# A graph network on one core: where an attention stage keeps its target rows and its masks, and how its head loads

## The chip, the cores and the metric

The program runs on one core of a Trainium2 chip, as one launch. Its time is the device time of that launch in microseconds, and three timed runs stand for it. The engines that matter are TensorE (PE, with its weight loads PEld), VectorE (DVE), ScalarE (ACT), GpSimd (POOL) and SyncE (SP). Each works through its own instructions in order; they meet in semaphores. Here POOL does nothing but issue row gathers by index, and SP and ACT also issue the other transfers. [...]

## What is computed

Two graph layers over 12,500 nodes of 128 features and 400,000 edges sorted by target. The first is a relational convolution of two sub-layers with ten relations, the second an attention layer with four heads of 32 features:

```python
h = jnp.maximum(_layernorm(x, axis=-1), 0.0)
x = x + _L0_gnn_ref(h, node_vec, edge_weight, edge_attr_42, ...)   # two relational sub-layers
h = jnp.maximum(_layernorm(x, axis=-1), 0.0)
x = x + _L1_gnn_ref(h, edge_index, W_l, W_r, att, bias)

def _L1_gnn_ref(x, edge_index, W_l, W_r, att, bias):
    xl, xr = (x @ W_l).reshape(n, H, C), (x @ W_r).reshape(n, H, C)
    xj, xi = xl[src], xr[dst]
    score = jnp.einsum('ehc,hc->eh', leaky_relu(xi + xj, 0.2), att)
    ex = jnp.exp(score - segment_max(score, dst)[dst])
    alpha = ex / (segment_sum(ex, dst)[dst] + 1e-16)
    out = segment_sum(alpha[..., None] * xj, dst)
    return out.reshape(n, H * C) + bias
```

All of it is in float32.

## The kernel before

The edges are cut into G = 125 groups of 3200: 128 partitions with J = 25 consecutive edges each. As the targets are sorted, a group touches at most 128 neighbouring nodes, and a half row (13 or 12 edges, `HALVES`) at most two of them. A check in the head confirms this, and a flag chooses between `sorted_edges` (which runs here) and a general path. The stages follow one another:

- **Head** (`first_table`, lines 327 to 449): 98 tiles of 128 nodes. Each is normalised, turned, and multiplied by the ten relation weights in three matmul groups; DVE copies the first and third part out of PSUM, ACT the second, and ACT's queue stores 640 KB per tile to the table `t1_d`. The rows of x come as 26 loads `xq` of four tiles (line 349), each into a tile of its own, and all are issued on SP's queue at the start, with the whole target list `dst_i` after the fourth (354) and the whole source list `src_i` after the seventh (356). Per four tiles, SP also stores `xb` (x plus a bias, two buffers, 445 and 446) and `hT`. From tile LEAD = 12 on, one step of `analysis` (185 to 325) goes into each tile; it reads `dst_i`.
- **Relational sub-layers** (`layer1`, `layer2`): per group, 25 gathers on POOL and sums on DVE and ACT.
- **Attention** (lines 871 to 1096): a loop of turns t = 0 to G, in an order that is written out by hand (`manual_schedule`). A turn works on three groups: it loads for group t, scores group a = t-1, and sums group q = t-3.

In an attention turn the order of issue is: 25 gathers `xs` (479) of group t, into one of five buffers; on SP `load(t)`: a cell of the target list (473), from it the row number, then the 128 target rows `xr` (906), the rows `db` (908), the penalties `pen` (910), and `x2` (1051). Then the first two `first_xr` copies `z` on ACT (931). `score(0)` on DVE: a predicated copy (937) that puts a partition's second target row over the first where the mask `mk` says so, the sum with the gathered rows (939), leaky relu times attention (941), and the reduction to scores (943). `flow` on DVE and PE carries maxima across partitions (967 to 982). `score(1)`; `end` finishes group q-1 and SP stores it (1020 to 1027). `add_up` takes maxima off the scores (988 to 994), exponentiates on ACT (998), and then for each of five slices of five edges: the product `xw` on DVE (1002), a small copy of the weights on ACT (1005), the one-hot `s` on DVE (1007), five matmuls into `po` (1011). `score(2)`, `score(3)`; `maxima` (949 to 960). Then `prepare(t)`: DVE compares `db` into `st` (916) and makes the masks `mk` (919), ACT copies `pk` (922), PE makes the target rows `xn` from `xr` and `st` (925). Last `take`: ACT copies the finished sums out of `po` (1036).

The places matter. `xn` is one PSUM bank, written by PE and read by both ACT (931) and DVE (937). `z` has two buffers in PSUM. One further bank, `bank`, holds the index row `iotap` that the one-hots compare with, and the two `exps` that ACT writes and DVE (1002) and ACT (1005) read. `mk` lies in SBUF. `xw` and `s` have four buffers each (pool "go", line 878), with five tiles of each per turn.

Of the kernel before, what the change touches and what calls it, by code (L numbers as in the profile page):

```python
# [18 lines left out]
P = 128  # L19
J = 25  # L20
# [6 lines left out]
def kernel(  # L27
# [299 lines left out]
    def first_table():  # L327

        Q = 4
        LEAD = 12  # L330
# [5 lines left out]
        with tc.tile_pool(name="vw", bufs=1) as wp, tc.tile_pool(name="vx", bufs=1) as xp, \  # L336
# [5 lines left out]
            b2b = bcast_row(wp, b2, "b2b")  # L342
            dst_i = ap.tile([P, G, J], I32, name="dst_i")
            xs = []
            for q, ts in enumerate(quads):
                n = len(ts)
                r = starts[ts[0]]
                xq = xp.tile([P, Q, D], F32, name=f"xq{q}")
                nc.sync.dma_start(xq[:, :n, :], x[r:r + n * P, :].rearrange("(k p) d -> p k d", p=P))
# [57 lines left out]
            for i in range(3):  # L407
                norm(i)
            for i in range(2):
                turn(i)  # L410
                relu(i)
            look = analysis(ap, pp, dst_i)
            for i, (q, k) in enumerate(tiles):
                hT = hTs[q][:, k, :]
                ts = tp.tile([P, R * D], F32, name="ts")

                def part(c):
                    n = min(512, R * D - c)
                    ps = psum.tile([P, 512], F32, name="ps")
                    nc.tensor.matmul(ps[:, :n], hT, wall[:, c:c + n], start=True, stop=True)  # L420
# [5 lines left out]
                nc.vector.tensor_copy(*one)  # L426
                nc.scalar.copy(*more[0])
                relu(i + 2)
                scales()
                norm(i + 3)  # L430
                for m in more[1:]:
                    nc.vector.tensor_copy(*m)
                n = len(quads[q])
                stats(q + 2, k)
                if k == n - 1:
                    for kk in range(n, Q):
                        stats(q + 2, kk)
                if i >= LEAD:
                    next(look, None)
                r = starts[quads[q][k]]  # L440
                nc.scalar.dma_start(tv[r:r + P, :], ts)
                if k == n - 1:
                    r = starts[quads[q][0]]
                    xb = xp.tile([P, Q, D], F32, name=f"xb{q % 2}")
                    nc.vector.tensor_add(xb[:, :n, :], xs[q][:, :n, :], b2b[:, None, :].to_broadcast([P, n, D]))
                    nc.sync.dma_start(xb_d[r:r + n * P, :].rearrange("(k p) d -> p k d", p=P), xb[:, :n, :])
                    nc.sync.dma_start(hT_d[:, r:r + n * P], hTs.pop(q)[:, :n, :].rearrange("d k p -> d (k p)"))
            for _ in look:
                pass


    def sorted_edges():
# [4 lines left out]
        with tc.tile_pool(name="sd", bufs=1, space=DRAM) as sd, tc.tile_pool(name="sk", bufs=1) as sk:  # L457
# [403 lines left out]
            with tc.tile_pool(name="gk", bufs=1) as kp, tc.tile_pool(name="gx", bufs=5) as xp, \  # L861
                    tc.tile_pool(name="gw", bufs=2) as wp, tc.tile_pool(name="gs", bufs=3) as sp, \
                    tc.tile_pool(name="go", bufs=4) as op, \
# [7 lines left out]
                exps = [bank[:, k * P:k * P + H * J].rearrange("p (h j) -> p h j", h=H) for k in (1, 2)]  # L871
                nc.vector.tensor_copy(iotap, iota)
# [20 lines left out]
                def flat(t):  # L893
                    return t.rearrange("p h j -> p (h j)")
# [18 lines left out]
                def prepare(g, xr, db):  # L913
# [3 lines left out]
                    mk = wp.tile([P, J], F32, name="mk")  # L917
# [8 lines left out]
                    return xn, mk.bitcast(I32), flat(pk)  # L926
# [69 lines left out]
                def sums(g, xs, sc, po, before):  # L996
# [3 lines left out]
                    for j0 in range(0, J, JW):  # L1000
                        xw = op.tile([P, JW, H, AW], F32, name="xw")
# [4 lines left out]
                        s = op.tile([P, JW, P], F32, name="s")  # L1006
                        nc.vector.tensor_tensor(s, iotap[:, None, :].to_broadcast([P, JW, P]),  # L1007
                                                dst_b[:, g, j0:j0 + JW, None].to_broadcast([P, JW, P]),
                                                op=OP.is_equal)
# [32 lines left out]
                with tc.manual_schedule():  # L1042
                    for t in range(G + 1):
# [33 lines left out]
                        score(1)  # L1077
                        if q >= 1:
                            end(q - 1)
# [7 lines left out]
                        if t < G:  # L1087
                            xn[t] = prepare(t, xr.pop(t), dbs.pop(t))
# [440 lines left out]
```

## Time and profile before

| | us |
|---|---|
| median of three runs | 14032.24 (14024.25 to 14067.41) |
| the profiled execution, its own time | 14041.59 |
| its span, first to last instruction | 14039.8 |
| head, 0 to about 283 | 283 |
| first sub-layer, 283 to 4893 | 4610 |
| second sub-layer, 4893 to 9340 | 4447 |
| attention, 9340 to 14040 | 4700 |
| one attention turn (from one first predicated copy at 11622.84 to the next at 11659.18) | 36.34 |

In a row of the timeline stand the start in us from the beginning of the span, the duration, the engine, the line, the operation with what it writes and reads, how many are merged, and in brackets the idle time before it with what ended it. "issue" and "remote" there mean that the profile doesn't show what ended the wait. A wait's row gives the engine and line that waited, what for, the total in us, how often, and the longest. Rows of a stretch give the busy time of each engine in it. The ends of matmuls are modelled.

### The profile page before, as it was taken

The page shows a single profiled execution, that of the slowest core. Times are in us where ns is not written, and L with a number is a line of the kernel's source. Part 1 is how long each engine was busy: PE and PEld are TensorE (multiplying, and loading weights), DVE is VectorE, ACT ScalarE, POOL GpSimd, SP SyncE. Part 2 cuts the span into 40 slices and gives each one's busy share as a digit, 9 for nine tenths or more (in the row PEclk, how much of TensorE's full clock was granted, in tenths as well). Part 3 has the DMA queues.
Part 4 walks back from the last instruction along what each step waited for, and adds up shares of the span by engine and source line. Part 5 has one row for each costly group of instructions (what it writes and reads, how often), then busy time and mean ns, then how long its engine had stood idle before and what let it go on. Part 6 is the DMA issues. An engine that isn't in the chain of part 4 may idle for free.

```text
span 14039.8 us, 68433 instructions
## 1 busy us (share of the span) xinstructions
PE 3446.7 (25%) x12832; PEld 2310.3 (16%) x12832; DVE 9212.9 (66%) x12638; ACT 2298.5 (16%) x6975; POOL 9120.0 (65%) x9384
## 2 busy tenths in 40 slices
PE   6122222222222211111111111112333333333333
PEld 3011111111111100000000000002222222222223
DVE  7566666666666565555555565656777777777777
ACT  2233223333232200000000000001111111111111
POOL 1666666666666577777777666655666666666664
PEclk8555555555555555555555555555666666666666
DMA  8222222222222211111111111111222222222221
GB/s 274 76 82 85 84 81 86 83 83 86 85 81 86 70 56 54 54 54 54 54 54 54 53 55 54 55 49 50 56 56 57 56 56 57 56 52 56 57 56 40
DMA packets 595938, 964.56 MB, mean 69 GB/s; under 512 B 190432, under 2 KB 397866, under 8 KB 595498
## 3 DMA queue, kind: packets, MB, share of 16 engines
q0 software_dynamic: 300000, 621.40, 16.5%
q1 hardware_dynamic: 280090, 273.82, 6.2%
q10 hardware_dynamic: 15408, 64.89, 1.2%
q14 instruction: 336, 2.75, 0.1%
q8 instruction: 104, 1.70, 0.0%
HBM read 758.60 MB, written 200.85 MB: 68 GB/s over the span
## 4 chain that ended last, share of the span: by engine, by line
issue 28%; DVE 27%; POOL 19%; another core or an unknown queue 12%; PE 6%; ACT 5%; DMA 2%; SPq 0%; DVEq 0%; ACTq 0%; POOLq 0%
POOL xs L496 14%; POOL xs L479 5%; ACT y L528 3%; DVE z L939 2%; DVE lr L941 2%; DVE y L516 2%; PE po L1011 2%; DVE xw L1002 2%; DVE sc L943 2%; DVE r L534 2%; DVE z L937 2%; DVE s L1007 1%; DVE r L519 1%; DMA xs<-xl_d,src_i 1%
## 5 line engine op out<-in xcount | busy, mean ns | idle before, releaser
L496 POOL DMA_INDIRECT xs<-t_d,idx x6250 | 6146.7, 983 | 2821.1 <-issue 1867.4
L479 POOL DMA_INDIRECT xs<-xl_d,src_i x3125 | 2971.4, 951 | 1690.9 <-issue 913.0
L519 DVE TENSOR_REDUCE r<-y 128x256 f32<-128x3072 f32 (+1 forms) x375 | 2102.9, 5608 | 30.5 <-DVE y L516 0.5
L516 DVE TENSOR_TENSOR y<-xs,wk 128x3072 f32<-128x3072 f32 (+1 forms) x375 | 1324.4, 3532 | 368.5 <-DMA xs<-t_d,idx 237.0
L1011 PE MATMUL po<-xw,s 128*128 128x132 f32 x6250 | 1101.5, 346 | 1323.5 <-issue 1030.4
L1011 PEld LDWEIGHTS po<-xw,s 128*128 128x128 f32 x6250 | 1019.5, 252 | 1385.8 <-issue 1054.3
L553 PE MATMUL ps<-r,s 128*128 128x128 f32 x1000 | 305.6, 461 | 3528.0 <-issue 1905.8
L714 PE MATMUL pt<-wall,hT 128*128 128x512 f32 x750 | 640.9, 991 | 1391.0 <-remote 865.0
L807 DVE TENSOR_TENSOR x<-sm,ac 128x128 f32<-128x128 f32 x125 | 36.4, 291 | 1420.0 <-DMA xl_d<-ts 1030.5
L528 ACT ACTIVATE y<-xs,wk 128x128 f32<-128x128 f32 x3000 | 933.6, 488 | 148.4 <-issue 92.2
L937 DVE COPY_PREDICATED z<-mk,xn 128x896 f32<-128x896 int32 x500 | 491.1, 982 | 561.5 <-ACT z L931 284.2
L553 PEld LDWEIGHTS ps<-r,s 128*128 128x128 f32 x1000 | 231.9, 322 | 3654.9 <-issue 1974.7
L1002 DVE TENSOR_TENSOR xw<-xs,bank 128x640 f32<-128x640 f32 x625 | 508.9, 814 | 304.4 <-remote 164.0
L1007 DVE TENSOR_TENSOR s<-bank,dst_b 128x640 f32<-128x640 f32 x625 | 515.4, 825 | 170.0 <-issue 89.9
L931 ACT COPY z<-xn 128x896 f32<-128x896 f32 x500 | 395.0, 812 | 909.7 <-DVE lr L941 689.8
L939 DVE TENSOR_TENSOR z<-xs,z 128x896 f32<-128x896 f32 x500 | 497.8, 996 | 39.3 <-DMA xs<-xl_d,src_i 22.4
L941 DVE SCALAR_TENSOR_TENSOR lr<-z,att 128x896 f32<-128x896 f32 x500 | 495.2, 990 | 17.1
L943 DVE TENSOR_REDUCE sc<-lr 128x28 f32<-128x896 f32 x500 | 493.9, 988 | 17.1
L553 PE MATMUL ps<-s,r 128*128 128x128 f32 x1000 | 305.5, 461 | 806.6 <-issue 433.3
L718 DVE TENSOR_TENSOR ts<-pt,xb 128x128 f32<-128x128 f32 x125 | 35.5, 284 | 697.6 <-ACT tr L650 649.5
L714 PEld LDWEIGHTS pt<-wall,hT 128*128 128x128 f32 x750 | 209.8, 320 | 1701.9 <-remote 942.9
L534 DVE TENSOR_REDUCE r<-y 128x256 f32<-128x3072 f32 x125 | 411.9, 3295 | 0.0
(211 smaller groups left out, 5834.7 us busy)
## 6 DMA issues: line engine op xcount, KB each, us to landing
xs<-t_d,idx POOLq DMA_INDIRECT x6250
t_d<-ts SPq DMA_DIRECT2D x125, 640.0 KB
m<-in_edge_attr_dram SPq DMA_DIRECT2D x125, 525.0 KB
t_d<-ts ACTq DMA_DIRECT2D x98, 640.0 KB
xs<-xl_d,src_i POOLq DMA_INDIRECT x3125
db<-drow_d SPq DMA_DIRECT2D x125, 128.0 KB
xl_d<-ts SPq DMA_DIRECT2D x125, 66.0 KB
at<-hT_d SPq DMA_DIRECT2D x125, 64.0 KB
```

What stands on the lines that cost most here:

```text
L479: nc.gpsimd.indirect_dma_start(out=xs[:, j, :], out_offset=None, in_=table, in_offset=bass.IndirectOffsetOnAxis(ap=ids[:, j:j + 1], axis=0))
L496: nc.gpsimd.indirect_dma_start(out=x[:, j, :], out_offset=None, in_=table, in_offset=bass.IndirectOffsetOnAxis(ap=ids[:, j0 + j:j0 + j + 1 ...
L516: nc.vector.tensor_mul(y[:, :, :n, :], xs[:, None, :n, :].to_broadcast([P, 2, n, D]), wk[:, :, :n, None].to_broadcast([P, 2, n, D]))
L519: nc.vector.tensor_reduce(r, y[:, :, :n, :].rearrange("p c j d -> p c d j"), AX.X, OP.add)
L528: nc.scalar.activation(y[:, c, :, j], xs[:, j, :], AF.Copy, scale=wk[:, c, j:j + 1])
L553: nc.tensor.matmul(ps, a, b, start=(k == 0 and c == 0), stop=(k == 1 and c == 1), skip_group_check=True)
L714: nc.tensor.matmul(pt[:, :n], hT, wall[:, c:c + n], start=True, stop=True)
L939: nc.vector.tensor_add(z, xs[:, j0:j0 + n, :D], z)
L941: nc.vector.scalar_tensor_tensor(lr[:, :n, :], z, 0.0, att8[:, None, :].to_broadcast([P, n, D]), op0=OP.max, op1=OP.mult)
L943: nc.vector.tensor_reduce(sc[:, :, j0:j0 + n].rearrange("p h j -> p j h"), lr[:, :n, :].rearrange("p j (h c) -> p j h c", h=H), AX.X, OP.add)
L1002: nc.vector.tensor_mul(xw[:, :, :, :C], xs[:, j0:j0 + JW, :D].rearrange("p j (h c) -> p j h c", h=H), ex[:, j0:j0 + JW, :, None].to_broadc ...
L1011: nc.tensor.matmul(po, s[:, j, :], xw[:, j].rearrange("p h a -> p (h a)"), start=(j0 + j == 0), stop=(j0 + j == J - 1), skip_group_check=True)
```

## The change

In the attention stage:

- `prepare(t)` moves from behind `maxima` to between `score(1)` and `end(q-1)`, in mid turn. This moves `st`, both `mk`, `pk` and the four `xn` matmuls; it issues no transfer.
- ACT copies `xn` to a new SBUF tile `xt` (two buffers); the `z` copies and the predicated copy read `xt` instead of `xn`.
- `mk` moves from SBUF into a free part of `bank`, behind the `exps`.
- In each slice the one-hot `s` is issued ahead of the product `xw`.
- `xw` and `s` get five buffers instead of four.

In the head: eight rotating buffers for x, with six loads at the start and then one for every four tiles; both lists come in eight pieces of 32 groups, one at the start of every fourth tile; the first three normalisations and two turns come ahead of the second quad's statistics; the bias row and two small zero stores go behind that; `analysis` starts at tile 8 instead of 12; `xb` has four buffers.

```diff
-        LEAD = 12
+        LEAD = 8
+        AHEAD = 6
...
-            b2b = bcast_row(wp, b2, "b2b")
             dst_i = ap.tile([P, G, J], I32, name="dst_i")
-            xs = []
-            for q, ts in enumerate(quads):
-                n = len(ts)
-                r = starts[ts[0]]
-                xq = xp.tile([P, Q, D], F32, name=f"xq{q}")
-                nc.sync.dma_start(xq[:, :n, :], x[r:r + n * P, :].rearrange("(k p) d -> p k d", p=P))
-                xs.append(xq)
-                if q == 0:
-                    nc.scalar.dma_start(wall.rearrange("d (r o) -> d r o", r=R), w_rel1.rearrange("r d o -> d r o"))
-                if q == min(3, len(quads) - 1):
-                    nc.sync.dma_start(dst_i, dstv)
-                if q == min(6, len(quads) - 1):
-                    nc.sync.dma_start(src_i, srcv)
-            nc.sync.dma_start(hT_d[:, NP - P:], zero[:, :P])
-            nc.sync.dma_start(xb_d[NP - P:, :], zero[:, :D])
+            xs = {}
+
+            def load_x(q):
+                if q < len(quads):
+                    n = len(quads[q])
+                    r = starts[quads[q][0]]
+                    xs[q] = xp.tile([P, Q, D], F32, name="xq")
+                    nc.sync.dma_start(xs[q][:, :n, :], x[r:r + n * P, :].rearrange("(k p) d -> p k d", p=P))
+
+            GC = 32
+            lists = [(a, b, g, min(g + GC, G)) for a, b in ((dst_i, dstv), (src_i, srcv)) for g in range(0, G, GC)]
+
+            def load_list():
+                if lists:
+                    a, b, g0, g1 = lists.pop(0)
+                    nc.sync.dma_start(a[:, g0:g1, :], b[:, g0:g1, :])
+
+            nc.scalar.dma_start(wall.rearrange("d (r o) -> d r o", r=R), w_rel1.rearrange("r d o -> d r o"))
+            for q in range(AHEAD):
+                load_x(q)
...
             for i, (q, k) in enumerate(tiles):
+                if k == 0:
+                    load_list()
+                    load_x(q + AHEAD)
...
-                    tc.tile_pool(name="go", bufs=4) as op, \
+                    tc.tile_pool(name="go", bufs=5) as op, \
...
+                others = [bank[:, k * P + H * J:k * P + (H + 1) * J] for k in (1, 2)]
...
-                    mk = wp.tile([P, J], F32, name="mk")
+                    mk = others[g % 2]
...
                     for k in range(4):
                         nc.tensor.matmul(xn[:, k, :], st[:, k, :], xr, start=True, stop=True)
-                    return xn, mk.bitcast(I32), flat(pk)
+                    xt = wp.tile([P, 4, D], F32, name="xt")
+                    nc.scalar.copy(xt, xn)
+                    return xt, mk.bitcast(I32), flat(pk)
...
                     for j0 in range(0, J, JW):
+                        s = op.tile([P, JW, P], F32, name="s")
+                        nc.vector.tensor_tensor(s, iotap[:, None, :].to_broadcast([P, JW, P]),
+                                                dst_b[:, g, j0:j0 + JW, None].to_broadcast([P, JW, P]),
+                                                op=OP.is_equal)
                         xw = op.tile([P, JW, H, AW], F32, name="xw")
...
                         nc.scalar.copy(xw[:, :, :, C], ex[:, j0:j0 + JW, :])
-                        s = op.tile([P, JW, P], F32, name="s")
-                        nc.vector.tensor_tensor(s, iotap[:, None, :].to_broadcast([P, JW, P]),
-                                                dst_b[:, g, j0:j0 + JW, None].to_broadcast([P, JW, P]),
-                                                op=OP.is_equal)
...
                         score(1)
+                        if t < G:
+                            xn[t] = prepare(t, xr.pop(t), dbs.pop(t))
                         if q >= 1:
                             end(q - 1)
...
                             sms[a], ros[a] = maxima(xs[a], scs[a], pks[a])
-                        if t < G:
-                            xn[t] = prepare(t, xr.pop(t), dbs.pop(t))
```

More of the change, by code (lines that the diff above doesn't have):

```diff
@@ L335, in first_table @@
         tiles = [(q, k) for q, ts in enumerate(quads) for k in range(len(ts))]
-        with tc.tile_pool(name="vw", bufs=1) as wp, tc.tile_pool(name="vx", bufs=1) as xp, \
+        with tc.tile_pool(name="vw", bufs=1) as wp, tc.tile_pool(name="vx", bufs=AHEAD + 2) as xp, \
                 tc.tile_pool(name="vh", bufs=4) as hp, tc.tile_pool(name="vt", bufs=4) as tp, \
@@ L406, in first_table @@
                 scales()
[L407 to L411, printed above, removed]
+                if q == 0:
+                    for i in range(3):
+                        norm(i)
+                    for i in range(2):
+                        turn(i)
+                        relu(i)
+            b2b = bcast_row(wp, b2, "b2b")
+            nc.sync.dma_start(hT_d[:, NP - P:], zero[:, :P])
+            nc.sync.dma_start(xb_d[NP - P:, :], zero[:, :D])
             look = analysis(ap, pp, dst_i)
             for i, (q, k) in enumerate(tiles):
+                if k == 0:
+                    load_list()
+                    load_x(q + AHEAD)
                 hT = hTs[q][:, k, :]
@@ L443, in first_table @@
                     r = starts[quads[q][0]]
-                    xb = xp.tile([P, Q, D], F32, name=f"xb{q % 2}")
+                    xb = hp.tile([P, Q, D], F32, name="xb")
                     nc.vector.tensor_add(xb[:, :n, :], xs[q][:, :n, :], b2b[:, None, :].to_broadcast([P, n, D]))
@@ L447, in first_table @@
                     nc.sync.dma_start(hT_d[:, r:r + n * P], hTs.pop(q)[:, :n, :].rearrange("d k p -> d (k p)"))
+            while lists:
+                load_list()
             for _ in look:
```

## The prediction

> **What bounds the kernel now.** I read the busy time by stage first, then the longest waits of the attention stage, then the timeline of one of its turns, engine by engine, and last the head. The stages:
>
> ```profile
> core 0: us, PE busy (x) PEld busy (x) DVE busy (x) ACT busy (x) POOL busy (x), PEclk, DMA share, GB/s
> 283.00:4893.00 4610.00, 1126.44 (x2503) 551.26 (x2503) 2837.56 (x4263) 1365.42 (x4249) 2968.43 (x3128) 0.53 0.27 83
> 4893.00:9340.00 4447.00, 535.56 (x1623) 318.74 (x1623) 2635.31 (x2255) 142.12 (x502) 3179.23 (x3124) 0.50 0.19 54
> 9340.00:14040.00 4700.00, 1547.62 (x7998) 1318.64 (x7998) 3533.93 (x5499) 707.04 (x2001) 2971.35 (x3125) 0.62 0.22 54
> ```
>
> The two middle stages aren't touched, so 4700 us of attention and 283 us of head are what can move. In the attention stage DVE is the busiest engine with 75%, and still a quarter of it is idle. Waits between 11000 and 12000 us, 27.5 turns:
>
> ```profile
> POOL xs L479 <- DVE xw L1002: 141.4, 27, 5.5
> DVE z L937 <- issue: 98.5, 28, 3.5
> DVE xw L1002 <- remote: 55.6, 27, 2.3
> ACT z L931 <- PE xn L925: 38.1, 28, 1.5
> ```
>
> POOL waits 5.2 us a turn for DVE's last product, which frees a gather buffer: POOL follows DVE. DVE stops twice a turn, 3.5 us ahead of the first predicated copy and 2.1 us ahead of the fifth product. One turn, DVE, ACT and POOL together:
>
> ```profile
> 11654.63 0.34 DVE L900 TENSOR_TENSOR_SCAN dn<-pk,sc 128x100 f32<-128x100 f32 x1
> 11654.89 0.50 DVE L916 TENSOR_SCALAR st<-db,pcol 128x512 f32<-128x512 bf16 x1
> 11659.18 1.10 DVE L937 COPY_PREDICATED z<-mk,xn 128x896 f32<-128x896 int32 x1 [3.52 <-issue]
> 11671.21 0.82 DVE L1002 TENSOR_TENSOR xw<-xs,bank 128x640 f32<-128x640 f32 x1 [0.38 <-issue]
> 11672.29 0.82 DVE L1007 TENSOR_TENSOR s<-bank,dst_b 128x640 f32<-128x640 f32 x1 [0.26 <-ACT xw L1005]
> 11680.68 0.82 DVE L1002 TENSOR_TENSOR xw<-xs,bank 128x640 f32<-128x640 f32 x1 [2.12 <-remote]
> ...
> 11655.94 0.25 ACT L1036 COPY su<-po 128x132 f32<-128x132 f32 x1
> 11657.55 1.59 ACT L931 COPY z<-xn 128x896 f32<-128x896 f32 x2 [1.35 <-PE xn L925]
> ...
> 11675.53 0.94 POOL L479 DMA_INDIRECT xs<-xl_d,src_i  x1 [0.30 <-issue]
> 11681.77 0.95 POOL L479 DMA_INDIRECT xs<-xl_d,src_i  x1 [5.30 <-DVE xw L1002]
> ```
>
> At the turn's end everything stands in a row: scan `dn`, then `st`, then the xn matmuls (from 11655.44, 2.08 us), then both z copies on ACT, then the predicated copy. It starts at 11659.18, when the second z copy has ended (11657.55 + 1.59), though it needs the first alone: ACT's second copy and DVE both read xn.
>
> **The turn, part by part.** Offsets are from the first predicated copy, 11659.18; a turn is 36.34 us.
>
> Turn's end. With xn made in mid turn, ACT goes from `su` straight to z. `pk` lay between `ro` (11655.48) and `su`; where the next copy follows at once ACT starts it 0.27 after `ro`, so su starts at 11655.75 and z about 0.16 later. One z copy of 896 takes 0.89, and the predicated copy waits for one only, as DVE and ACT now share no bank there: 11655.91 + 0.89 + 0.04 = 11656.84 instead of 11659.18. **Saves 2.34.** About 1.9 us stay idle behind `dn`, with ACT's `ro` and z the last to be ready. Reading xt from SBUF instead of PSUM should not lengthen z: the copy `ke` from SBUF to PSUM takes 392 ns for 275 elements, the copy `ts` from PSUM 376 for 260.
>
> Mid turn. `st` and the masks take 11654.89 to 11655.66 at the old place and the same behind score(1). **Costs 0.77.** The rest of prepare is on other engines. Score(1) ends at offset 9.21. TensorE starts xn 0.55 after `st` and takes 2.08: 11.84. ACT's copy `xt` of 128x512 out of PSUM takes 586 ns (the head's `ts` copy): 12.45. Queued behind it on ACT is the exponential. Its scores were ready at 11.65 and now are at 11.65 + 0.77 = 12.42; so the exponential is held by 0 to 0.1 us, and I take none. Nothing else on ACT is due; TensorE idles there. The rows that `prepare` needs: SP issues `db` at 11678.48, offset 19.3, for the next turn, and now needs it at the next turn's 9.21, with turns of 32.6 at 41.8. The store of `o` ahead of it in SP's queue comes 0.8 later than before. Some 19 us of cover remain, so this costs nothing.
>
> The slices. DVE could have gone on to the fifth product at 11678.56 and started at 11680.68; by the same wait in another turn (12226.27) TensorE's po ended it, so what is waited for is one of four buffers. With five, each tile waits for the matmul of a turn ago. **Saves 2.12**; nothing is late next on TensorE, which has till the end of the turn. One-hot first: the first one-hot takes the place of the first product, and the 0.38 us for the exponential could be covered, the five waits of 0.26 to 0.32 too, 1.7 us in all. But the trace says that one-hots wait for ACT's small copy, whose output they don't read; what the two have in common is `bank`. The exponential writes that bank. So I take that all these waits stay: one-hot, product, small copy, next one-hot, at the old 1.81 us a slice. Behind the fifth product the predicated copy of score(2) waits for the small copy, as its mask now lies in that bank, where before the fifth one-hot did. Five slices take 9.05 instead of 11.35 less 2.12. **Saves 0.1** (0 to 1.8).
>
> [...]
>
> The masks. Writing 13 elements to PSUM: the row `wk` there in the sub-layers has 236 ns against 216 to 221 for `mk` now; two of them, 0.04. The predicated copy with mask in PSUM and data in SBUF has no row. Before it had one operand in each, now also; the sum L939, SBUF with PSUM into PSUM, takes 1.095 for 896 against 1.085. I take no change; the ends are -0.1 and +0.4 a turn, a tenth on four copies.
>
> Sum of a turn: 36.34 - 2.34 + 0.77 - 2.12 - 0.1 = **32.55 us**. POOL's limit must lie under that: 24 gathers in a row ran from 11609.04 to 11639.18 (one issued every 1.256), 25 make 31.4. It does, by 1.1 us, so POOL still waits. Full turns are t = 4 to 124, 121 of them: 121 x 3.79 = **459 us**. The last, short turn and the two sums behind it have one fifth product each: 6. The first turns run while gathers are awaited: nothing.
>
> **The head.** Tile by tile it runs at 2.26 us, 98 tiles, 221 us; it takes 283. The loss lies early:
>
> ```profile
> 25.98 40.99 SPq L349 DMA_DIRECT2D xq<-in_x_dram  x19
> ...
> 49.49 0.69 DVE L426 COPY ts<-ps 128x512 f32<-128x512 f32 x1 [12.09 <-PE ps L420]
> 73.01 0.69 DVE L445 TENSOR_TENSOR xb<-xq,b2b 128x512 f32<-128x512 f32 x1 [11.05 <-DMA xb_d<-xb]
> ```
>
> SP issues loads until 67 us, and the store of `xb` that DVE waits for stands behind them. Spread out, these waits go; but the transfers remain, and the table's stores keep the DMA engines at a share of 0.79 to 0.94 after 80 us. The first 80 us had shares of 0.99, 1.17, 1.06 and 1.07, 86 us of full work, of which 12 tiles at 2.26 x 0.86 are 23: the loads are worth some 62. The first tile's copy out of PSUM starts at 17.6. All hidden, 17.6 + 221 + 2 = 241, 42 us are saved; none hidden, the head takes 62 more than that 239, 301, and loses 18. Nearest is the middle, as the lists fall into the first 32 tiles, which are full: **-12 us**. Analysis reads a piece of `dst_i` eight or more tiles after its load, 18 us; SP's other queue entries come in the same order as now.
>
> Sum: 14041.6 (the profiled execution, of which 1.8 lies around the span) - 459 - 6 - 12 = 13564.6. It was 9.4 over the median, so 13555; I say 13560.
>
> **The rivals.**
>
> 1. ACT gets in the way: the exponential comes late behind xt, or the first predicated copy still waits for both z copies (0.75). For: ACT is in order, and xt and the scores meet within 0.1 us. Against: only 2.6 us of TensorE and 0.6 of ACT lie before. At 0.8 to 2 us a turn: 13,650 to 13,800.
> 2. POOL becomes the bound: one of the bank waits goes after all and DVE drops below 31.4. 121 x 4.94 = 598: about 13,415.
> 3. The fifth product's wait isn't for a buffer ("remote" names no one) and stays: 121 x 2.12 back, 13,815. Against: the row in which TensorE ends it.
> 4. Slower than before: TensorE's issue. In the attention stage's third turn it took its instructions one in 1.4 us, and DVE stood:
>
> ```profile
> 9553.83 1.10 DVE L937 COPY_PREDICATED z<-mk,xn 128x896 f32<-128x896 int32 x1 [98.00 <-ACT z L931]
> ```
>
> A second such stretch, from 12337, made one turn 60.60. I don't know what starts them; POOL was gathering without a pause, which denser turns make more common. With 98 us each, five more of them eat the 477 and the sixth makes it slower: 14,060 and up. Against: two in 125 turns.
> 5. The change doesn't do what it says in time: something else in the turn takes up the 3.8 us, within 42 us of now. Against: each engine but DVE and POOL is idle for more than half of the turn.
>
> **How the numbers follow.** Forecast 0.60; ACT 0.14; POOL 0.08; the fifth product 0.05; a gain still smaller, 13,830 to 13,990, 0.04; no change 0.02; TensorE's issue slower 0.07. A difference under 0.3%, 42 us, can't be told from none here. Faster: 0.60 + 0.14 + 0.08 + 0.05 + 0.04 = 0.91; same 0.02; slower 0.07. The forecast's own range takes the head (-30 to +30) and 0.4 us a turn: 13,500 to 13,620. For eight in ten it takes in rivals 1 and 2 as well: 13,400 to 13,800, 0.18 left out.
>
> **What would show it.** First predicated copy: idle near 1.9 instead of 3.5, its wait ending with a single z copy. Fifth product: no wait. First one-hot: still 0.38 behind the exponential, each next one 0.26 behind ACT's small copy. POOL's wait for DVE: 1 us instead of 5.2. Turn: 32.5. xt ends within 0.1 of the scores. Head: xb's wait gone, SP's issues spread, last tile near 270. It is wrong where DVE waits in mid turn for `db` or the exponential, where the predicated copy takes over 1.2 us, or where more stretches of one instruction per 1.4 us show on TensorE.

## The result, and where the time went

The changed kernel took 15231.06 us (median of four runs, 15227.94 to 15242.00), the kernel before 14028.24 on the same chip: a ratio of 1.0853, 95% interval 1.0832 to 1.0875. The forecast was 13560. The profiled execution took 15242.0 us with a span of 15240.2. Its stages, cut 24 us earlier than those of before because the head ends earlier:

```profile
core 0: us, PE busy (x) PEld busy (x) DVE busy (x) ACT busy (x) POOL busy (x), PEclk, DMA share, GB/s
259.00:4869.00 4610.00, 1126.23 (x2501) 550.98 (x2501) 2837.45 (x4261) 1370.09 (x4249) 2965.69 (x3127) 0.53 0.29 83
4869.00:9316.00 4447.00, 536.07 (x1625) 319.21 (x1625) 2636.75 (x2256) 141.89 (x502) 3181.06 (x3125) 0.50 0.21 54
9316.00:15240.00 5924.00, 1682.30 (x7998) 1393.77 (x7998) 3536.52 (x5499) 783.77 (x2126) 2949.15 (x3125) 0.58 0.19 43
```

The head's last operation ended at 256.1 us instead of 280.6, the middle stages took what they took, and the attention takes 5924 us instead of 4700. DVE is busy there for 3536 us against 3534: it does the same work and waits 1220 us more. The longest waits between 11000 and 12000 us (the engine and line that waited, for what, us in total, how often, the longest):

```profile
POOL xs L494 <- DVE xw L1024: 330.1, 21, 28.5
DVE z L955 <- ACT z L949: 303.1, 21, 28.6
ACT ro L978 <- remote: 273.2, 10, 27.6
```

In 21 turns DVE waits at the first predicated copy for 303 us, behind ACT, and ACT waits ten times for 27 us ahead of its copy `ro`. So the loss is not spread: it sits in ten of 21 turns. From one first predicated copy to the next, the turns from the fourth on:

```
32.70 61.57 32.92 61.61 32.69 61.55 32.70 61.50 32.70 61.51 32.70 61.69 32.70 61.66 ...
120 turns: 59 of 32.7 to 35.6 (median 32.70), 57 of 61.65 in the mean, 4 of 40.4
```

Every second turn is the turn of the forecast, 32.70 against 32.55. A short one and the long one behind it, from the timeline:

```profile
12015.03 0.59 ACT L943 COPY xt<-xn 128x512 f32<-128x512 f32 x1 [2.59 <-PE xn L941]
12015.68 0.26 ACT L1016 ACTIVATE bank<-sc 128x100 f32<-128x100 f32 x1
12015.97 0.82 DVE L1020 TENSOR_TENSOR s<-bank,dst_b 128x640 f32<-128x640 f32 x1 [0.39 <-ACT bank L1016]
...
12017.66 0.36 SPq L926 DMA_DIRECT2D pen<-pen_d  x1
...
12023.27 0.82 DVE L1020 TENSOR_TENSOR s<-bank,dst_b 128x640 f32<-128x640 f32 x1 [0.26 <-ACT xw L1027]
12025.08 1.10 DVE L955 COPY_PREDICATED z<-bank,xt 128x896 f32<-128x896 int32 x1 [0.26 <-ACT xw L1027]
12025.09 0.94 POOL L494 DMA_INDIRECT xs<-xl_d,src_i  x1 [28.08 <-DVE xw L1024]
...
12034.49 0.36 ACT L978 COPY ro<-px 4x256 f32<-4x256 f32 x1 [0.93 <-PE px L976]
12035.84 1.10 DVE L955 COPY_PREDICATED z<-bank,xt 128x896 f32<-128x896 int32 x1 [1.86 <-ACT z L949]
...
12056.91 0.71 SPq L926 DMA_DIRECT2D pen<-pen_d  x1
12058.58 0.82 DVE L1020 TENSOR_TENSOR s<-bank,dst_b 128x640 f32<-128x640 f32 x1 [1.24 <-issue]
12060.40 0.94 POOL L494 DMA_INDIRECT xs<-xl_d,src_i  x1 [4.38 <-DVE xw L1024]
...
12069.34 0.42 PE L976 MATMUL px<-ident,dn 128*4 128x128 f32 x1
...
12090.35 0.94 POOL L494 DMA_INDIRECT xs<-xl_d,src_i  x1 [0.30 <-issue]
12096.07 0.36 ACT L978 COPY ro<-px 4x256 f32<-4x256 f32 x1 [27.20 <-remote]
```

In the short turn POOL stands still (28.08 us) while TensorE does its 25 matmuls; all waits are those that the forecast named: 0.39 for the exponential, 0.26 for each small copy, none ahead of the fifth slice, 1.86 for a single z copy. In the long turn POOL gathers through the matmuls but for one pause of 4.38 us. TensorE's last matmul of the turn, for `px`, ends at 12069.76 by the model, but ACT, which waits for it, goes on at 12096.07, 4.8 us after POOL's last gather. An update here is a recorded step of TensorE's semaphore: `ro` starts 0.02 us after the one at 12096.05. TensorE's updates in that turn, against the matmuls that they belong to (the ends are modelled; between `xn`'s matmuls and ACT's copy `ro` eight are due and eight are recorded):

```
po, 1st to 5th slice: matmuls end 12053.5, 12055.3, 12057.2, 12061.6, 12066.9
                      updates     12061.96, 12066.31, 12075.50, 12093.09, 12095.94
ecol, px, px:         updates     12095.98, 12096.01, 12096.05
```

They come 8 to 31 us after the modelled ends, the first three while POOL still gathers and the last four within 0.11 us, when POOL has run out of buffers. Whether the matmuls end so late or only their updates come so late isn't shown: their starts are on record, their ends aren't. Other engines are slowed in that stretch too: SP's issue takes 0.71 us where it takes 0.36 in the short turn, and its register moves 0.70 instead of 0.03. As POOL then stands dry for 28 us, the next turn is short, POOL starts again at its end, and the one after is long.

### The profile page after: what moved, and what is told of

Its sections match the earlier page's. It is cut to its first block, busy times and chain, and to the rows that moved or that the text cites. A ratio compares the mean times of both kernels' runs of the same rounds, so it can differ in the third digit from the quotient of the medians.

```text
span 15240.2 us, 69068 instructions
## 1 busy us (share of the span) xinstructions
PE 3578.2 (23%) x12832; PEld 2384.2 (16%) x12832; DVE 9217.7 (60%) x12638; ACT 2379.7 (16%) x7100; POOL 9096.9 (60%) x9384
## 4 chain that ended last, share of the span: by engine, by line
DVE 28%; issue 26%; another core or an unknown queue 18%; POOL 15%; ACT 6%; PE 4%; DMA 2%; DVEq 0%; ACTq 0%; SPq 0%; POOLq 0%
POOL xs L511 14%; DVE xw L1024 3%; ACT y L543 3%; DVE y L531 3%; DVE z L957 3%; DVE lr L959 2%; DVE z L955 2%; DVE sc L961 2%; DVE r L534 2%; DVE r L549 1%; DMA xs<-xl_d,src_i 1%; POOL xs L494 1%; DVE u L649 1%; PE ps L433 1%
## 5 line engine op out<-in xcount | busy, mean ns | idle before, releaser
L955 DVE COPY_PREDICATED z<-bank,xt 128x896 f32<-128x896 int32 x500 | 493.7, 987 | 1897.6 <-ACT z L949 1851.1
L1029 PE MATMUL po<-xw,s 128*128 128x132 f32 x6250 | 1224.4, 355 | 989.9 <-issue 719.2
L1029 PEld LDWEIGHTS po<-xw,s 128*128 128x128 f32 x6250 | 1093.5, 258 | 1104.8 <-issue 801.9
L822 DVE TENSOR_TENSOR x<-sm,ac 128x128 f32<-128x128 f32 x125 | 36.4, 291 | 1417.9 <-DMA xl_d<-ts 1095.0
L949 ACT COPY z<-xt 128x896 f32<-128x896 f32 x500 | 404.0, 822 | 647.6 <-DVE lr L959 362.2
```

Of the source, the lines that this page charges most:

```text
L1029: nc.tensor.matmul(po, s[:, j, :], xw[:, j].rearrange("p h a -> p (h a)"), start=(j0 + j == 0), stop=(j0 + j == J - 1), skip_group_check=True)
```

## Experiments

Theory 1, gathers: TensorE's updates are held while POOL gathers without a pause beside the 25 matmuls; four buffers stop DVE, DVE's stop stops POOL, and in that pause the updates come. Theory 2, updates: as DVE no longer reads TensorE's `xn` itself, it waits for each slice's matmuls, and TensorE sends 11 updates a turn instead of 7 (the matmuls of two turns carry 22 in the changed kernel's trace and 14 in that of before; by the programs, the read of `xn` covered four of the five slices before). Theory 3, loads: SP's loads land among the matmuls. Ratios are to the kernel before on the same chip. The runs came to several chips; its median lies between 14,028 and 14,254 us on them, but for the last three runs.

**Four buffers.** The rest is as in the changed kernel.

```diff
-                    tc.tile_pool(name="go", bufs=5) as op, \
+                    tc.tile_pool(name="go", bufs=4) as op, \
```

> Only the five buffers of the slices are undone; the rest of the change stays. Updates theory: what stalls every second turn is the number of semaphore updates that TensorE sends in its 25 matmuls; after the change every fifth matmul sends one (11 in a turn, before 7), because DVE no longer reads TensorE's own output and so waits for each tile's matmuls by itself. With four buffers there are still 11, so turns of some 61 us stay: 15,150 to 15,300 us. Gathers theory: the stall comes where TensorE's matmuls run while POOL gathers without a pause; with four buffers DVE stops 2.1 us at the fifth slice, turns take 34.8, POOL pauses over 3 us in each, and the stalls go: 13,700 to 13,850 us.

Measured: 14001.81 us, ratio 0.987 (0.981 to 0.993). No turn is long; 119 of 120 are near 37.0. The fifth buffer makes the loss. But the gathers theory had 34.8: the turn is some 31 us of gathers and a pause of 6.1, and DVE, which was to wait 2.1 us at the fifth slice, waits 3.9 in the mean. Both waits between 11000 and 12000 us:

```profile
POOL xs L494 <- DVE xw L1024: 164.5, 27, 6.4
DVE s L1020 <- remote: 100.8, 26, 4.7
```

**One wait instead of five.**

```diff
+                            if t < G:
+                                seen = wp.tile([P, 1], F32, name="seen")
+                                nc.vector.tensor_copy(seen, xn[t][3][:, 3, 0:1])
```

> The changed kernel, plus one small DVE copy per turn (128 x 1 out of xn, behind less_maxima). By it DVE has waited for TensorE once in the turn, the five waits ahead of the one-hots need no semaphore of their own, and TensorE sends 6 updates in a turn instead of 11, one instead of six in the 25 matmuls and the one behind them. Buffers, order, gathers and transfers stay. Updates theory: no slow turns, all take 32.7 to 33.0 us: 13,430 to 13,530 us. Gathers theory: POOL gathers through the matmuls as before, every second turn stays at about 61.6 us: 15,200 to 15,300 us.

Measured: 14453.59 us, ratio 1.016 (1.010 to 1.022). With one update in place of six, 35 of 120 turns are still long (61.2 us), 14 take some 40, the rest 32.6 to 36.4. The counts are of the longest of the four runs, 14684.63 us; the other three took 14334 to 14455. So the number of updates isn't the cause; it has a part in how often.

**Prepare at the turn's end again.**

```diff
                         score(1)
-                        if t < G:
-                            xn[t] = prepare(t, xr.pop(t), dbs.pop(t))
...
                             sms[a], ros[a] = maxima(xs[a], scs[a], pks[a])
+                        if t < G:
+                            xn[t] = prepare(t, xr.pop(t), dbs.pop(t))
```

> Only the move of prepare is undone: it stands behind maxima again; xt, masks in the bank, order and five buffers stay. Updates theory: still 11 updates in a turn, so long turns stay: 15,150 to 15,500 us. Gathers theory: turns of 34 to 36 us leave POOL a pause of 3 to 4 us in each, no long turns: 13,650 to 13,950 us.

Measured: 15178.56 us, ratio 1.070 (1.064 to 1.076): 59 long turns of 59.7, 61 of 34.12. This went as the updates theory said and against the number that I gave for the gathers; but with five buffers DVE doesn't stop here either, so my figure for the pause was the error. The move isn't the cause.

**The new head alone, on the kernel before.**

> The kernel before with the new head alone. The first predicated copy of the attention came at 9325.0 us after the change and at 9348.9 before: the head's part is a gain of about 24 us, 13,995 to 14,015 us, and nothing else moves. The forecast had 12 us, 14,015 to 14,025. If the gain ahead of the attention is not the head's: 14,025 to 14,035.

Measured: 14161.73 us beside 14161.18, ratio 0.997 (0.994 to 1.001): not resolved, as on this chip the runs of both spread, over 258 and 188 us. The profile shows why: 11 of 120 attention turns are 59 us long (in the profile of before it was one), without any change there. The head itself is clear: its last operation ends at 258.1 us instead of 280.6. In all 18 profiles with the new head it ends between 254.5 and 258.9, in the two with the old one at 280.4 and 280.6.

**SP's loads behind the matmuls; and no loads.** In the first, `end(q - 1)` moves behind `score(3)`; in the second, the four loads are made once.

```diff
-                        if q >= 1:
-                            end(q - 1)
...
                         score(3)
+                        if q >= 1:
+                            end(q - 1)
```

> The changed kernel with one thing moved: a group's finish (DVE L1038 to L1043, then SP's store of the output and behind it SP's loads for the next group) stands behind score(3) instead of ahead of the slices, so that SP's five issues and their transfers land behind the matmuls of the slices and not among them. Loads theory (the stall comes where SP's loads, POOL's gathers and the 25 matmuls meet): no turns of 61 us, all 32.7, 13,400 to 13,550 us. Gathers theory (matmuls of the slices against gathers without a pause, whatever SP does): long turns stay, 15,150 to 15,300 us.

> The changed kernel without the four loads of a turn on SP: target rows, comparison rows, penalties and x2 are those of the first group for all; the cell of the target list, the row number and the output's store stay. Loads theory: all turns 32.7: 13,400 to 13,550 us. Gathers theory: 25 gathers in a row remain, and every second turn stays near 61 us: 15,150 to 15,300 us.

Measured: 15283.23 (ratio 1.088) and 15266.5 us (1.087). Both alternate like the changed kernel, 33.36 and 61.2, 32.70 and 61.6. These loads have no part in it.

**Thirteen gathers instead of 25.**

```diff
+                    for j in range(0, J, 2):
+                        nc.gpsimd.indirect_dma_start(
+                            out=rows[t % 5][:, j, :], out_offset=None, in_=xl_d[:N, :],
```

> The changed kernel with 13 gathers a turn instead of 25 in the attention (every second one; the rows of the others are left as they stand, so scores and sums are not the layer's). POOL then needs 16.3 us of a turn and pauses for half of it. Gathers theory: no turns of 61 us, all 32.7: 13,350 to 13,550 us. Loads theory or a theory of the change's other parts (order, updates, mask in the bank): every second turn stays near 61 us: 15,000 to 15,300 us.

Measured: 13709.46 us, ratio 0.976 (0.973 to 0.979). No turn is long, but nearly all are 34.6 to 34.9, not 32.7. The timeline shows the missing 2 us to be the same stall, cut short:

```profile
11406.34 0.94 POOL L1055 DMA_INDIRECT rows<-xl_d,src_i  x1 [18.77 <-DVE xw L1024]
...
11421.35 0.95 POOL L1055 DMA_INDIRECT rows<-xl_d,src_i  x1 [0.30 <-issue]
11422.59 0.42 PE L976 MATMUL px<-ident,dn 128*4 128x128 f32 x1
11425.10 0.36 ACT L978 COPY ro<-px 4x256 f32<-4x256 f32 x1 [2.99 <-remote]
```

The 13 gathers begin with the matmuls and end at 11422.30, and ACT, which waits for TensorE's `px`, goes on 2.8 us later.

**Ten matmuls instead of 25.**

```diff
-                        for j in range(JW):
+                        for j in (0, 4):
```

> The changed kernel with 2 of 5 matmuls in each slice (10 instead of 25 in a turn; three fifths of the sums are left out). TensorE then sends more updates in a turn, not fewer: 19 instead of 11, one per matmul. Theory that it is the length of TensorE's run of matmuls beside the gathers: no turns of 61 us, all 32.7: 13,400 to 13,550 us. Updates theory: more updates make it worse, turns of 61 us and more stay: 15,200 us or above. Gathers or loads alone, without TensorE's part in it: unchanged, 15,150 to 15,300 us.

Measured: 14439.15 us, ratio 1.028 (1.025 to 1.031). From the fifth turn on, as the stall of the first turns reaches into the fourth here, there are 13 turns over 50 us, 44 of some 44 and 63 of 32.7 to 36.2. Three fifths fewer matmuls take away about half of what the long turns cost (120 turns take 4811 us instead of 5609; at 32.7 each they would take 3924), though updates rise from 11 to 19. So the length of TensorE's run of matmuls has a part, but ten don't end the stalls.

**Five buffers alone, on the kernel before.**

```diff
-                    tc.tile_pool(name="go", bufs=4) as op, \
+                    tc.tile_pool(name="go", bufs=5) as op, \
```

> The kernel before with five buffers of the slices instead of four, and nothing else. DVE then doesn't stop for TensorE in mid turn, and TensorE sends 7 updates instead of 8, one behind all 25 matmuls and not one in their midst. By the forecast's step a turn is 36.34 - 2.12 = 34.2: 13,760 to 13,790 us. Gathers theory: what DVE's stop gave was POOL's pause, in which TensorE's update came; without it every second turn waits some 26 us for POOL to run dry, 34 and 60 us in turn: 14,900 to 15,300 us.

Measured: 15169.4 us, ratio 1.064 (1.059 to 1.069). 59 turns of 59.2 alternate with 61 of 34.06. Its waits between 11000 and 12000 us are those of the changed kernel:

```profile
POOL xs L479 <- DVE xw L1002: 310.8, 12, 28.3
DVE z L937 <- ACT z L931: 284.1, 10, 28.7
ACT ro L960 <- remote: 270.9, 10, 27.2
```

So on such a chip one number in one line makes the loss, with 6 updates of TensorE a turn where the kernel before has 7 (the expectation counts one too many in both). That settles the place, and Theory 2 falls.

**Slices spread over the turn; short rows; half of the rows.** The first puts score(2) and score(3) between slices; the others keep 25 gathers a turn and make each smaller.

```diff
-                        score(2)
-                        score(3)
+                            add_up(q, io, [lambda: score(2), lambda: score(3)])
```

```diff
-                        out=xs[:, j, :], out_offset=None, in_=table,
+                            out=rows[t % 5][:, j, :SHORT], out_offset=None, in_=short_d[:N, :],
```

```diff
-                        out=xs[:, j, :], out_offset=None, in_=table,
+                            out=rows[t % 5][:P // 2, j, :], out_offset=None, in_=xl_d[:N, :],
```

> The changed kernel with the slices spread over the turn: two slices, score(2), two slices, score(3), the fifth. TensorE's 25 matmuls then take some 18 us instead of 9; their number, buffers and gathers stay. If it is how densely matmuls follow one another beside the gathers: no long turns, 32.7 to 33.5 each, 13,400 to 13,600 us. If it is how many there are beside gathers without a pause: long turns of some 61 us stay in every second turn, 15,100 to 15,400 us. Between (as with 10 matmuls a turn): 14,300 to 14,700 us.

> The changed kernel with 25 gathers a turn of 128 rows each as before, but from a table with rows of 128 bytes (all zero) instead of 528, so that a quarter of the bytes moves; POOL's instructions and the number of rows stay, scores and sums are not the layer's. If the bytes in flight are what holds TensorE's updates: no long turns, 13,400 to 13,600 us. If it is the number of gathers and of their rows: long turns stay, 15,100 to 15,400 us.

> The changed kernel (five slice buffers) with 25 gathers a turn that fetch 64 rows each instead of 128 (the other half of the partitions keeps zeros, so scores and sums are not the layer's). If the number of rows counts: stalls shrink or go, as with 13 gathers, 13,400 to 14,300 us. If the number of POOL's gathers counts and they still take some 1.25 us each: long turns stay, 15,000 to 15,700 us.

Measured: 15441.67 (ratio 1.083), 15696.11 (1.101) and 15699.96 us (one run, ratio 1.107 to the median beside it). Spreading helps nothing: 52 turns of 66.8. With a quarter of the bytes, or half of the rows, nearly every turn is long, 51.2 and 51.3: gathers of 0.95 and 0.90 us, one issued every 1.25 and 1.20. So moving less didn't end the stalls. Thirteen gathers in a row instead of 25 did: by their number, or by the time that POOL takes over them (25 take 30 to 31 us in all three, 13 take 16); these two aren't told apart.

**Four buffers, and the product first.** In the run with four buffers the pause ends with the fifth product, which stood behind the one-hot that waits.

```diff
-                        s = op.tile([P, JW, P], F32, name="s")
...
                         nc.scalar.copy(xw[:, :, :, C], ex[:, j0:j0 + JW, :])
+                        s = op.tile([P, JW, P], F32, name="s")
...
-                    tc.tile_pool(name="go", bufs=5) as op, \
+                    tc.tile_pool(name="go", bufs=4) as op, \
```

> The changed kernel with four buffers and the product ahead of the one-hot again (head, prepare's place, xt and the masks in the bank stay). With four buffers alone turns took 37.0 us and none was long: 31.4 of gathers and a pause of 6.1 that ends with the fifth slice's product, which there stands behind the one-hot that waits. With the product first it ends 0.75 us sooner: turns of 36.2 to 36.3, none long, 90 us less than with four buffers alone, ratio to the kernel before 0.985 to 0.995. If long turns return now and then, as in the kernel before: ratio 0.99 to 1.01.

Measured: 13899.49 us (13887.30 to 13908.26, six runs), ratio 0.975 (0.973 to 0.978). 118 of 120 turns take 35.7 to 36.4 us (median 36.2) and none is long. The waits between 11000 and 12000 us:

```profile
POOL xs L494 <- DVE xw L1020: 143.0, 28, 5.2
DVE xw L1020 <- remote: 89.1, 28, 3.4
DVE z L955 <- issue: 50.3, 27, 1.9
```

POOL's pause is 5.1 us, 5.2 before the change (141.4 in 27), and the turn is much the same too. DVE waits 1.9 us at the first predicated copy where it waited 3.5, and 3.2 at the fifth product where it waited 2.1: most of what prepare's move saved it now waits at the other place.

**Four and six buffers of gathered rows.** On that version, `gx` with four and with six instead of five.

> The version with four slice buffers and the product first, with four buffers of gathered rows instead of five. POOL then fills four buffers in a row at the attention's start, not five, and stops 25 gathers, 31.3 us, sooner. If the stall of the third turn ends with that row: the third period (142.1 us with five) is 111, the steady turns stay 36.2, 30 us less in all. If that stall has a length of its own: 142 as now, and no gain. If POOL needs the fifth buffer in the steady turns: turns above 36.3.

> The same with six buffers of gathered rows. If the third turn's stall ends with the row of gathers that fills the buffers: its period is 173 us instead of 142.1. If it has a length of its own: 142. The steady turns stay 36.2 in both.

Measured: the third turn's period is 107.5 with four, 142.1 with five, 159.5 with six; POOL's first row of gathers ends 86.8, 118.2 and 149.1 us into it. The steady turns are 36.2 in all. With four 13900.61 us (ratio 0.979, 0.974 to 0.984), with six 13952.25 (one run). The third turn's stall, which every kernel had, the one before too, ends after POOL's row, 20.6, 23.9 and 10.4 us after it; that lag isn't constant, and I have no reading for it. Run by run the 35 us drown in the chips' spread.

**ScalarE instructions added.** Thirty tiny copies a turn on the version with four buffers and the product first, among the slices and away from them.

```diff
                         nc.scalar.copy(xw[:, :, :, C], ex[:, j0:j0 + JW, :])
+                        for _ in range(6):
+                            nc.scalar.copy(spare, lows)
```

> The version with four slice buffers and the product first, and six tiny ScalarE copies (4 x 1) behind each small copy of the slices, 30 in a turn, where ScalarE idles 1.6 us between its small copies. Shared-path theory (TensorE's updates wait behind all instructions of all engines): the slices' stretch gets denser by 30 instructions, POOL's pause of 5.1 us grows and turns are longer than 36.2 by 1 us or more, or long turns return. Theory of TensorE and POOL alone: 36.2 to 36.6 as without them.

> The same version with the 30 tiny copies away from the slices: ten behind the copy of io, twenty behind score(2), both in stretches in which ScalarE idles. Shared-path theory with a backlog over the whole turn: turns longer than 36.2 by 1 us or more, here too. Shared-path theory with a limit in the slices' stretch alone, or TensorE and POOL alone: 36.2.

Measured: 12286.69 and 12295.20 us, and the kernel before took 12503.09 beside them. Neither theory had that. This was another chip, and on it nothing stalls: the turns are 32.6 and 32.7, the third is 38.5, SP's moves take 0.03 us among the slices, and the attention's first predicated copy comes at 8170 us instead of 9230 to 9350, so the sub-layers, which no version touches, are over a thousand us faster too. What the 30 copies were to tell apart they can't tell here.

**The change again, beside the kernel before.**

> The changed kernel as it is, once more. In the last two runs the kernel before took 12503 us, where every other measurement gave 14,000 to 14,300, and no turn was long, though POOL gathered without a pause: SyncE's moves took 0.03 us and not 0.7, TensorE's updates came at once. If the chip is again such a one, the changed kernel's turns are all 32.6 to 32.7 as the forecast had them, and it takes 12,250 to 12,320 us beside 12,500. If it is one like the others, every second turn is 61 us again and the ratio 1.08 to 1.09.

Measured: 12298.15 us (12296.10 to 12300.00, four runs) beside 12491.51 (12488.61 to 12497.70, seven runs), ratio 0.984 (0.983 to 0.986). The same program that is 8.5% slower than the kernel before on one chip is 1.6% faster than it on another. One turn there:

```profile
10046.79 0.82 DVE L1020 TENSOR_TENSOR s<-bank,dst_b 128x640 f32<-128x640 f32 x1 [0.38 <-ACT bank L1016]
10049.42 0.38 SPq L926 DMA_DIRECT2D pen<-pen_d  x1
10055.91 1.10 DVE L955 COPY_PREDICATED z<-bank,xt 128x896 f32<-128x896 int32 x1 [0.26 <-ACT xw L1027]
10055.92 0.94 POOL L494 DMA_INDIRECT xs<-xl_d,src_i  x1 [1.57 <-DVE xw L1024]
10066.66 1.10 DVE L955 COPY_PREDICATED z<-bank,xt 128x896 f32<-128x896 int32 x1 [1.86 <-ACT z L949]
```

POOL gathers through the slices, with a pause of 1.57 us, and still TensorE's updates for the five slices come at 10051.26, 10053.06, 10054.19, 10055.53 and 10057.34, as the matmuls end. All 120 steady turns are 32.7 to 33.1. So gathers almost without a pause are a condition of the stall on some chips, not a cause by themselves.

## Why the prediction was wrong

- **Turn's end, -2.34: right.** One z copy is waited for, and the idle time is 1.86 us, forecast near 1.9.
- **Mid turn, +0.77, and no wait behind xt: right.** xt ends 0.06 us ahead of the exponential's start, and the first one-hot waits 0.39.
- **"Saves 2.12; nothing is late next on TensorE": this step failed.** TensorE's matmuls start early enough, but the updates that the others wait for come late. In the two turns shown, those of the slices come within 0.02 us of the modelled ends where POOL pauses for 28.08 us, and 8 to 31 us late where it pauses for 4.38. Before, POOL paused because DVE stopped, and DVE stopped for one of four buffers. The fifth buffer took that chain apart, POOL's pause in the slices fell from 5.2 us to 2.5 to 4.5, and nearly every second turn pays some 29 us, 27 of them ahead of `ro`. The sum: 57 x 28.95 and 4 x 7.7 are 1681, less 120 x 3.65 = 438 for the shorter turns, 24 for the one long turn that was there before, and 24 for the head: +1195. Measured: +1200 (15242.0 less 14041.6).
- **"POOL waits 5.2 us a turn: POOL follows DVE": the reading under it.** The wait was read as slack of POOL. It was a part of the turn: 31.1 of gathers and 5.2 of pause are the 36.3, and with four buffers no saving on DVE moved it (36.2 with prepare moved). The sign was in the rows that I showed: when the fifth product's wait ended, at 11680.68, POOL had stood still for 4.2 us. And in the trace of before the last matmul of the first slice starts at 11675.31 (modelled end 11675.74) and its update comes at 11680.66: for five microseconds DVE's slice buffer waits on an update.
- **Slices, -0.1: right in size, wrong for another case.** The prediction's own figures, 11.35 less 2.12 less 9.05, give 0.18, ten us in all. From the first slice to the predicated copy behind the fifth, the short turn takes 9.11 us. The small copies' waits of 0.26 stay with either order. With four buffers one-hots first cost 0.8 us a turn (37.0 against 36.2), as POOL's buffer comes free behind the product.
- **Masks in the bank: nothing, right.** The predicated copy takes 987 ns in the mean, 982 before.
- **Head, -12: undersized.** It gained 24 us.
- **Rival 4** named the stall, "TensorE's issue", and that denser turns would bring more of it. It was priced by the 98 us of the first turns and given 0.07. The later one in the same profile, 60.60 us for a turn, was the one to price: 24 us each, and a cause that the change touches.
- **Without the stalls** the sum holds in part. On the last chip the turn is 32.7, forecast 32.55. There is no trace of the kernel before from there; by an estimate its turns are some 34.1: its span is 12489.7 us, the changed kernel's first predicated copy comes at 8165.8 and before would come 24 us later by its head, which leaves 4300 for the attention, less some 205 outside the 120 turns. That is the 34.06 to 34.12 of the short turns with prepare last. So the move gains some 1.4 us a turn (terms: -2.34 + 0.77 - 0.1 = -1.67). The fifth buffer gains nothing there: with four and the product first, the two runs with added copies had turns of 32.6 and 32.7 too.

## What to carry to other kernels

An idle engine that waits for the bottleneck can be part of a loop, as POOL with its 5.2 us a turn was here: before a stop is removed, ask what comes in during it, and look at when semaphores change, not only at when matmuls end. A wait that ended 5 us after the matmul that it was for (update at 11680.66, modelled end 11675.74) wasn't cured by another buffer alone: with five, the ratio was 1.064. And one long turn in a profile, or runs that spread, is a state that a change can make the rule: price the change in that state too, and on more than one chip.

For this kernel: four buffers and the product first, with the rest of the change, beat both kernels where turns stall (13899.49 us, ratio 0.975), and with the 30 idle copies took 12286.69 where they don't, beside 12503.09 for the kernel before (one run each).

## What was not expected of the hardware

- In the long turn shown, on the chip of the result, TensorE's updates from the slices on came 8 to 31 us after their matmuls' modelled ends while POOL issued gathers every 1.25 us; the last four came together, 4.7 us after POOL's last gather. All chips here but two had long turns. A single update outside the slices, for `xn`, was there at once (ACT went on 0.04 us after the matmul's end), though POOL gathered.
- On those chips it went by the number of gathers or POOL's time over them (with five slice buffers and 25 matmuls, 13 a turn: none long; 25: 35 of 120 turns with one wait, else some half or nearly all), not by their bytes (128 a row instead of 528: 15696.11 us, no better) or rows (64 instead of 128: 15699.96 us, no better).
- In those stretches several engines are slowed. In the long turn shown a register move of SyncE takes 0.70 us instead of 0.03, TensorE's matmuls in the slices start up to 1.68 us apart (in the short turn at most 0.38), DVE's one-hots wait 1.24 us; POOL keeps its 1.25 us a gather. Between 260 and 4800 us, long before the attention, 263 of 367 of SyncE's moves take over 0.5 us on the chip of the result, none of 405 on the last chip. Something that instructions of several engines pass would fit that; no run shows it. One more thing goes with the stalls: on the chips where turns stall, 42 to 57% of the updates of DVE's semaphore have no record (in the changed kernel's trace 5643 of 10582 have one), though in the head, in which POOL doesn't gather, none is missing (372 of 372 there up to 250 us); on the two chips without stalls none is missing at all. All executions here are recorded ones, so that no run shows whether the recording has a part in the stalls or only suffers from them, or what differs between the chips: this stays open.
- The changed kernel took 12298 and 15231 us on two chips, the kernel before 12492 and 14028. The mean granted clocks of TensorE for the changed kernel, 0.562 and 0.549, are 2% apart, the times 24%.
- The length of POOL's pause in the slices parts the turns. In the thirteen traces with 25 whole gathers a turn on such chips, from the fifth turn on and but for the last three, each long turn has a pause of at most 4.5 us or none, each turn under 37.5 us one of at least 4.3, and within a trace the two don't overlap. The 11 long turns with the new head alone have 2.4 to 3.7, its others 4.3 and more; the long turn of the kernel before has 3.95; the version with four buffers and the product first never falls under 4.8 and has no long turn. That is a count over the traces; no run sets the pause alone. What makes it short in those 11 turns, and why the turns part at some 4.4 us, isn't settled.
